# Graph attention in two layers: the store of mask bytes on another queue, a third buffer for it, and two statements moved

## The chip, the cores and the metric

The kernel runs on one core of one Trainium2 chip. The metric is the device time of one execution in microseconds (us); lower is better. Times below are medians of several executions, with the lowest and highest in brackets. PE is the matmul engine, DVE the vector engine, ACT the scalar engine, POOL is GpSimd, and SP is SyncE, which here only starts transfers.

## The reference, cut to what matters

There are 4096 rows of 512 numbers, and a dense 4096 x 4096 matrix `adj` in float32. Layer 0 attends within graphs of 128 rows, layer 1 over all pairs of rows where `adj > 0`.

```python
def _L0_gnn_ref(x, b, edge_encoding, ptr, Wq, bq, Wk, bk, Wv, bv):
    # b and edge_encoding are both adj
    mask = graph_id[:, None] == graph_id[None, :]
    a = jnp.where(mask, query @ key.T * scale, 0.0)
    scores = (a + b + edge_encoding) * jnp.where(mask, 1.0, -1000000.0)
    softmax = jax.nn.softmax(scores, axis=-1) * mask
    return softmax @ value
...
h = jnp.maximum(_layernorm(x), 0.0)
x = x + _L0_gnn_ref(h, adj, adj, ...)
h = jnp.maximum(_layernorm(x), 0.0)
x = x + _L1_gnn_ref(h, adj, ...)        # masks with adj > 0
```

So layer 0 needs from each row of `adj` the 128 entries of its own graph (`diag`) and a sum of exponentials over all the others (`sums`). Layer 1 needs from it one bit for each entry. The kernel reads `adj` once, in layer 0, and leaves the bits as bytes in memory (`a_d`) for layer 1.

## The kernel before

Layer 0 goes through 32 tiles of 128 rows, in pairs g = 0 to 15. `read` does all the work on a tile of `adj`: mask bytes on DVE and their store, `diag` on POOL, the sums on ACT, and the load of the tile three further on. L numbers in profile lines are lines of this kernel, or of the kernel profiled.

```python
def load_adj(pool, i):
    a = pool.tile([P, N], F32, name="a")                 # pool of 3
    nc.sync.dma_start(a, adj[ts(i, P), :])               # L104, 2 MB
...
def norm(src, hn):
    nc.vector.bn_stats(stats, src)                       # L111, "statistics"
    nc.vector.bn_aggr(mv, stats)
    ...                                                  # ve, rstd on POOL
    nc.vector.tensor_scalar(hn, src, mv[:, 0:1], rstd, ALU.subtract, ALU.mult)   # L118
...
def mask_bytes(pool, a, i):
    a8 = pool.tile([P, N], FP8, name="a8")               # pool of 2
    ...
    for u in range(P // B):                              # four operations
        nc.vector.tensor_scalar(a8v[:, u], av[:, u], 0.0, None, ALU.is_gt, saturate=False)  # L133
    nc.gpsimd.dma_start(a_d[i], a8.bitcast(F32))         # L136, 512 KB
...
def read(i, diag, sums):
    mask_bytes(sb, aa[i], i)
    nc.gpsimd.tensor_copy(diag, aa[i][:, ts(i, P)])      # L427
    for c0, c1 in ((0, i * P), ((i + 1) * P, N)):
        nc.scalar.activation(junk[:, c0:c1], aa[i][:, c0:c1], AF.Exp, scale=2.0 * NEG,
                             accum_out=sums[:, n : n + 1])               # L432
    if i + 3 < NT:
        aa[i + 3] = load_adj(ap, i + 3)
...
for g in range(NG):                                      # 16 pairs
    if g + 2 < NG:
        load_pair(g + 2)                                 # L489: xg, 512 KB, pool of 3
    if g == 2:
        w1x = load_w1(pool1, sb)                         # eight DVE operations
    ...
    def look_on(t):                                      # adj of the next pair
        if not last:
            i = G * (g + 1) + t
            nlook[2].append(read(i, nlook[0][:, t, :], nlook[1][t]))
    ...
    look_on(0)
    s = scores(g, hT, gT, r, *look)                      # PE L453, DVE L458, ACT L460
    prepare_on()
    prepare_on()
    if not last:
        ngT = queries(nhT)                               # PE L404, ACT L408
    look_on(1)
    sT = turned(s)                                       # PE L472, ACT L474
    for t in range(G):
        attend(sT, vs[t], g, t)                          # PE L480, DVE L482, ACT starts x's store
        prepare_on()
        if not last:
            nvs.append(values(nhT, t))                   # PE L416, DVE L420
    ...
    if g + 2 < NG:
        nhT, nr = normed(g + 2)                          # statistics, hn, PE L124, ACT L125 (hT)
```

The order of these statements isn't the order in which an engine runs them. The build, which turns this text into one list of instructions for each engine, chooses an order for each list; by what rule it chooses is not shown here.

## Time and profile before

| | kernel before |
|---|---|
| time (3 runs) | 1020.01 us (1017.76 to 1020.05) |
| span of the profiled run | 1017.6 us |
| layer 0, start of scores of pair 0 to pair 12 | 264.8 us |
| from the start of pair 15's scores to the end | 639.2 us |
| clock of PE granted in pairs 0 to 11 | 0.94 |

The page's chain of work that ended last, by engine:

```profile
PE 71%; DMA 12%; DVE 8%; ACT 4%; POOL 3%; issue 1%; ACTq 0%; SPq 0%; DVEq 0%; POOLq 0%
```

Nearly a third of the chain isn't PE, though PE is busy for 94% of the span. The work of PE is there, but at times something else holds it up, and for 12% of the span this chain waited for a transfer (DMA).

### The profile page before, as it was taken

How to read it: one execution, taken by the hardware profiler on the slowest of the kernel's cores; microseconds unless marked ns; L12 is line 12 of the kernel's file. 1: busy time of each engine (PE TensorE's matmuls, PEld its weight loads, DVE VectorE, ACT ScalarE, POOL GpSimd, SP SyncE). 2: the span in 40 equal slices, each digit the busy share in tenths (PEclk: the TensorE clock that was granted, in tenths of full speed). 3: DMA queues.
4: the chain of work that ended last, by engine and by line, in shares of the span. 5: the costliest groups of instructions: out<-in, count | busy, mean ns of one | idle time of the engine just before them, and what ended most of it. 6: DMA issues, size and time to landing. Idle time of an engine off the chain costs nothing.

```text
span 1017.6 us, 12962 instructions
## 1 busy us (share of the span) xinstructions
PE 961.5 (94%) x5051; PEld 826.3 (81%) x5051; DVE 452.8 (44%) x854; ACT 251.0 (25%) x441; POOL 197.2 (19%) x376
## 2 busy tenths in 40 slices
PE   7898889889898999899999999999999999999995
PEld 4475657556576667788899999999999999999995
DVE  3757756556555428755513323323323323323311
ACT  3774745555445212333310000000000000000000
POOL 1211133211112105555511001001001001001000
PEclk9799899999899999999999999999999999999998
DMA  9989988778774114222202123123123122122111
GB/s 354 395 346 365 364 308 308 297 314 300 282 272 166 52 57 130 81 65 65 61 1 84 47 78 83 47 79 83 47 79 83 47 78 84 47 78 82 44 42 34
DMA packets 53431, 148.25 MB, mean 146 GB/s; under 512 B 5874, under 2 KB 22514, under 8 KB 49266
## 3 DMA queue, kind: packets, MB, share of 16 engines
q1 hardware_dynamic: 38962, 113.52, 33.1%
q10 hardware_dynamic: 9792, 17.05, 4.5%
q0 software_dynamic: 4608, 16.78, 4.1%
q8 instruction: 41, 0.67, 0.3%
q14 instruction: 28, 0.23, 0.1%
HBM read 113.77 MB, written 33.55 MB: 145 GB/s over the span
## 4 chain that ended last, share of the span: by engine, by line
PE 71%; DMA 12%; DVE 8%; ACT 4%; POOL 3%; issue 1%; ACTq 0%; SPq 0%; DVEq 0%; POOLq 0%
PE pg L282 48%; PE pp L242 8%; DMA xg<-x 6%; PE pp L416 5%; PE pp L404 4%; DMA a_d<-a 3%; ACT junk L432 3%; DMA a<-adj 3%; PE pp L480 2%; DVE a L133 2%; DVE stats L111 2%; PE pt L124 1%; PE pp L188 1%; POOL rstd L117 1%; DVE x L482 1%
## 5 line engine op out<-in xcount | busy, mean ns | idle before, releaser
L282 PE MATMUL pg<-part,at 128*128 128x348 f32 x3072 | 489.0, 321 | 1.2 <-DVE e L251 1.2
L282 PEld LDWEIGHTS pg<-part,at 128*128 128x128 f32 x3072 | 488.7, 188 | 1.6 <-issue 1.6
L276 DVE CAST at<-at 128x4096 fp32r<-128x4096 fp8e4 x32 | 73.6, 2300 | 311.6 <-PE pg L282 311.6
L289 ACT COPY tot<-pg 128x522 f32<-128x522 f32 x32 | 19.1, 597 | 469.9 <-PE pg L282 469.9
L432 ACT ACTIVATE junk<-a 128x3968 bf16<-128x3968 f32 (+30 forms) x62 | 118.3, 1908 | 37.6 <-DMA a<-adj 21.3
L404 PE MATMUL pp<-hT,m_sb 128*128 128x256 f32 x512 | 118.7, 392 | 9.1 <-ACT hT L125 9.1
L416 PE MATMUL pp<-wv,hT 128*128 128x512 f32 x256 | 123.3, 627 | 2.5 <-ACT hT L125 2.5
L404 PEld LDWEIGHTS pp<-hT,m_sb 128*128 128x128 f32 x512 | 99.9, 198 | 23.9 <-ACT hT L125 9.5
L242 PE MATMUL pp<-w1x,hT 128*128 128x256 f32 (+1 forms) x512 | 118.5, 385 | 0.0
L416 PEld LDWEIGHTS pp<-wv,hT 128*128 128x128 f32 x256 | 51.8, 203 | 69.2 <-issue 66.3
L133 DVE TENSOR_SCALAR a<-a 128x1024 fp8e4<-128x1024 f32 x128 | 87.3, 745 | 46.1 <-DMA a<-adj 23.8
L242 PEld LDWEIGHTS pp<-w1x,hT 128*128 128x128 f32 x512 | 95.6, 192 | 14.0 <-issue 0.5
L582 POOL COPY den_all<-tot 128x1 f32<-128x1 f32 x31 | 5.7, 184 | 368.5 <-DVE tot L290 368.5
L125 ACT ACTIVATE hT<-pt 128x512 f32<-128x512 f32 x64 | 38.2, 600 | 118.1 <-PE pt L124 110.9
L591 POOL TENSOR_TENSOR tot<-tot,row 128x512 f32<-128x512 f32 x31 | 39.9, 1288 | 61.8 <-DVE tot L295 61.8
L480 PE MATMUL pp<-v,sT 128*128 128x512 f32 x64 | 36.8, 657 | 15.3 <-ACT sT L474 15.0
L230 POOL TENSOR_TENSOR part<-e,part 128x522 fp32r<-128x522 f32 x32 | 42.3, 1322 | 29.8 <-ACT part L229 26.2
L136 POOL DMA_DIRECT2D a_d<-a x32 | 22.0, 686 | 117.3 <-DVE a L133 108.1
L482 DVE SCALAR_TENSOR_TENSOR x<-pp,rs_all,xg 128x512 f32<-128x512 f32 x32 | 24.0, 750 | 41.7 <-PE pp L480 41.7
L115 POOL TENSOR_SCALAR ve<-mv 128x1 f32<-128x1 f32 x64 | 18.2, 287 | 121.2 <-DVE mv L113 119.5
L269 DVE STREAM_TRANSPOSE at<-mw 128x1024 f32<-128x1024 f32 x32 | 39.6, 1237 | 0.0
L117 POOL TENSOR_TENSOR rstd<-ve,neghalf 128x1 f32<-128x1 f32 x64 | 38.7, 607 | 3.9
(95 smaller groups left out, 596.6 us busy)
## 6 DMA issues: line engine op xcount, KB each, us to landing
a<-adj SPq DMA_DIRECT2D x32, 2048.0 KB, 11.8
a_d<-a POOLq DMA_DIRECT2D x32, 512.0 KB, 8.8
row<-x_d SPq DMA_DIRECT2D x64, 256.0 KB, 3.4
mw<-a_d SPq DMA_DIRECT2D x128, 128.0 KB, 3.9
xg<-x SPq DMA_DIRECT2D x16, 512.0 KB, 5.5
x_d<-x ACTq DMA_DIRECT2D x32, 256.0 KB, 4.8
out<-tot ACTq DMA_DIRECT2D x31, 256.0 KB, 3.8
wkT_sb<-wkT SPq DMA_DIRECT2D x4, 256.0 KB, 4.0
```

The source lines that it names most:

```text
L117: nc.gpsimd.tensor_tensor(rstd, ve, neghalf, ALU.pow)
L133: nc.vector.tensor_scalar(a8v[:, u], av[:, u], 0.0, None, ALU.is_gt, saturate=False)
L230: nc.gpsimd.tensor_sub(dst[:, :, 1, :], e3, dst[:, :, 0, :].bitcast(F32))
L242: nc.tensor.matmul(pm[g][:, :n], hT[:, k, :], w1x[:, k, g * HW : g * HW + n], start=(k == 0), stop=(k == KC - 1),)
L269: nc.vector.transpose(at8.rearrange("p c n b -> p (c n b)").bitcast(F32).rearrange("p (c u n) -> p c u n", c=NW, n=B), mw.rearrange("p u ( ...
L276: nc.vector.tensor_copy(at.rearrange("p (c b) q -> p c b q", b=BY), at8.rearrange("p c q b -> p c b q"))
L282: nc.tensor.matmul(pg[:, c, : 2 * CW1], at[:, j, :], part(j)[:, c].rearrange("p s w -> p (s w)"), start=(j == 0), stop=(j == NT - 1),)
L404: nc.tensor.matmul(pp[:, : G * P], m_sb[:, k, ts(m, P)], hT[:, k, :], start=(k == 0), stop=(k == KC - 1),)
L416: nc.tensor.matmul(pp, hT[:, k, ts(t, P)], wv[:, k, :], start=(k == 0), stop=(k == KC - 1))
L432: nc.scalar.activation(junk[:, c0:c1], aa[i][:, c0:c1], AF.Exp, scale=2.0 * NEG, accum_out=sums[:, n : n + 1],)
L480: nc.tensor.matmul(po, sT[:, t, :], v, start=True, stop=True)
L591: nc.gpsimd.tensor_add(num, num, row)
```

## The change

There are three edits. The mask bytes get a third buffer. SyncE starts their store in place of GpSimd. And the work on the coming pair's `adj`, which stood ahead of scores and ahead of the turned scores, is moved behind both, in front of the attends. It was meant to let scores and queries go first, and to keep a slow store from blocking the mask operations.

```diff
-        a8 = pool.tile([P, N], FP8, name="a8")
+        a8 = pool.tile([P, N], FP8, name="a8", bufs=3)
...
-        nc.gpsimd.dma_start(a_d[i], a8.bitcast(F32))
+        nc.sync.dma_start(a_d[i], a8.bitcast(F32))
...
-                    look_on(0)
                     s = scores(g, hT, gT, r, *look)
                     prepare_on()
                     prepare_on()
                     if not last:
                         ngT = queries(nhT)
-                    look_on(1)
                     sT = turned(s)
                     nvs = []
                     for t in range(G):
+                        look_on(t)
                         attend(sT, vs[t], g, t)
```

## The prediction

> **What bounds the kernel now.** I read the page first (busy tenths, chain that ended last), then busy time by stretch, then the timeline of PE through layer 0, then the waits and the chain around PE's gaps.
>
> Layer 0 works on pairs of row tiles. For each pair PE runs scores (L453), queries (L404), a transpose of the scores (L472), and twice attend (L480) plus values (L416). DVE turns adj into mask bytes (L133), ACT sums over adj (L432, "junk"). In PE's timeline the score blocks of pairs 0 to 15 start at 57.8, 77.7, 98.0, 124.7, 143.4, 169.2, 192.0, 212.9, 236.6, 255.4, 280.2, 299.5, 322.7, 341.4, 360.1 and 378.4 us. I cut there, at pair 12:
>
> ```profile
> core 0: us, PE busy (x) PEld busy (x) DVE busy (x) ACT busy (x) POOL busy (x), PEclk, DMA share, GB/s
> 57.84:322.65 264.81, 238.09 (x939) 159.16 (x937) 157.62 (x340) 147.72 (x239) 56.53 (x110) 0.94 0.80 306
> 322.65:378.58 55.93, 55.74 (x235) 37.95 (x234) 22.00 (x56) 12.17 (x33) 7.48 (x18) 1.00 0.18 62
> ```
>
> The last three pairs have all of adj on the chip and take 18.70, 18.70 and 18.37 us, PE never idle, clock 1.00. I take 18.7 as PE's floor for a pair. The first twelve take 264.8/12 = 22.1 us: PE has 26.7 us without work and a clock of 0.94, while DVE (60%), ACT (56%) and the DMA engines (80%) all have time left. So **no engine bounds this stretch; waits do**. Above the floor lie 264.8 - 12 x 18.7 = **40.4 us**. That is all the change can win here. What follows 378 us (layer 1, where L282 has PE at 99%) it does not touch.
>
> A pair at the floor, then two that stall (PE's timeline):
>
> ```profile
> 322.65 1.95 PE L453 MATMUL pss<-hT,gT 128*128 128x128 f32 x16
> 324.43 7.07 PE L404 MATMUL pp<-hT,m_sb 128*128 128x256 f32 x32
> ...
> 143.40 1.95 PE L453 MATMUL pss<-hT,gT 128*128 128x128 f32 x16
> 149.57 9.74 PE L404 MATMUL pp<-hT,m_sb 128*128 128x256 f32 x32 [4.22 <-ACT hT L125]
> ...
> 181.31 1.33 PE L480 MATMUL pp<-v,sT 128*128 128x512 f32 x2 [2.54 <-ACT sT L474]
> 182.43 5.13 PE L416 MATMUL pp<-wv,hT 128*128 128x512 f32 x8
> ```
>
> After a gap of 4.22 us the same 32 matmuls of L404 took 9.74 instead of 7.07 us, after 2.54 us L416 took 5.13 instead of 3.60: a gap is paid about one and a half times. The chain of waits tells where the two kinds come from:
>
> ```profile
> 136.64 10.38 DMA a_d<-a
> 147.01 0.03 DVEq L133
> 147.05 0.18 DVE a L133
> 147.22 0.57 DVE v L420
> 147.79 0.67 DVE x L482
> ...
> 148.92 0.60 ACT hT L125
> 149.57 9.75 PE pp L404 x32
> ...
> 165.59 0.76 DVE x L482
> 166.35 0.02 issue
> 166.37 5.64 DMA xg<-x
> 172.01 0.02 issue
> 172.03 1.29 DVE stats L111 x2
> ```
>
> Kind one: DVE stands in front of a mask operation until a store of mask bytes (10.4 us from its issue by POOL) frees one of two buffers; values, attend, ACT's x store and hT queue behind it. Kind two: in DVE's order the statistics of a coming pair (needing xg, loaded only when the last attend frees its buffer) stand ahead of this pair's scores (L458). Scores come 3 us late, ACT's exponentials and junk slide, and sT reaches PE late. The waits of this stretch put sizes to it:
>
> ```profile
> DVE a L133 <- DMA a_d<-a: 20.8, 6, 8.9
> DVE stats L111 <- DMA xg<-x: 15.3, 10, 3.5
> PE pp L480 <- ACT sT L474: 15.0, 9, 3.4
> PE pp L404 <- ACT hT L125: 9.1, 2, 4.9
> ```
>
> **What the Trainium skill says.** "TensorE: Matmul & The Clock Gate", Part 1: an idle window of about 3.4 us drops the array to half clock until it has been busy about as long; the trace agrees in kind (9.74 against 7.07 us), though there a gap of 2.54 us already cost 1.5. "DMA: Bandwidth & Descriptors", "Issuing engines are not separate DMA queues": DMAs of SP, ACT and GpSimd end on the same 16 engines, so the move to SyncE buys no bandwidth. The trace can only agree: stores and loads overlap there. Same page, "Where 436 GB/s comes from": a ceiling of 435 GB/s; the DMA view from 100 to 300 us has single slices up to 450. "Perfetto Trace Analysis", "Optimization Strategy": equal bubbles on the engine that should be full can mean too few buffers, which fits kind one.
>
> **The change, part by part.** No operation is added or removed; PE, DVE and ACT do the same layer-0 work. I compared the instruction order of both builds.
>
> (1) Third buffer for mask bytes. A store may now last until three tiles later, about 1.5 pairs or 28 us, against 2.5 to 12.3 us that stores take. I expect the 20.8 us of DVE waiting to fall under 3. Behind it lay pair 4 (excess 25.75 - 18.7 = 7.1 us) and parts of others.
>
> (2) The adj work behind scores and queries. Before, statistics stand ahead of the scores on DVE in 11 of the 13 pairs 1 to 13; after, in 3 (6, 11, 13). Before, masks run some four pairs ahead of the scores, so POOL's diag copy (three buffers) must wait for a score and the adj loads behind it with it (49.9 us of POOL waiting); after, two to three pairs. Also, the eight operations that build w1x stood before an attend of pair 1, which led to the other large hT stall (pair 2, from 98.0: 26.7 - 18.7 = 8.0 us); after, they follow that pair's attends.
>
> (3) Stores by SyncE. SyncE waits in order, so each store stands ahead of the adj load of its turn. That load needs the same masks done, so it loses nothing; but both stand behind the xg load, which waits for the last attend. From the order: at the attend (about 16.5 us after a pair's scores start) xg, store, load, store, load leave within 2 us. With the two x stores that is 2x2048 + 2x512 + 512 + 2x256 KB = 6144 KB = 6.29 MB a pair; at 390 GB/s (375 at share 0.96 in the first 50 us) 16 us, ending about 14 us into the next pair. The first load is needed about 11 us into that pair and lands at 5 to 7; the second at about 19.6 and lands by 14. Both fit, with 4 to 5 us to spare. At the floor the demand is 6.29 MB/18.7 us = 336 GB/s, under the 350 GB/s that the stretch 58 to 169 us moved.
>
> So what holds PE off its floor goes, and DMA stays just under it. I keep 8 us of the 40.4 for what I cannot see: three pairs with statistics still ahead (1 to 2 us each), w1x in pair 2 (1 us), first pairs and a DMA that runs tight (3 us). Prologue and layer 1: 0. **1020 - (40.4 - 8) = 988 us** (rounded).
>
> **Rivals.**
> - *The wait moves to adj.* For: DMA at 86% of its best rate, loads in one burst behind an in-order SyncE, masks less far ahead, so a late load hits scores sooner (junk stands ahead of the exponentials in several pairs). Against: 4 to 5 us of slack by my schedule. If pairs came at 20.4 us: 12 x (22.1 - 20.4) = 20 us, 1000 us.
> - *ACT stays the brake.* For: a junk operation of about 2 us still stands between the copies of queries and sT in most pairs, and at the floor ACT has 0.4 us between the last query copy and the transpose. Against: pairs 3 and 8 ran at 18.7 and 18.8 us with just such an order. A stall of 1 us in each pair: 996 us.
> - *SyncE's order hurts.* If stores hold back xg or a load holds back the next store, statistics come late and the old wait returns with new names: no gain, about 1015 us. Against: xg leaves first in each burst.
> - *The gain was in DMA alone and is hidden:* no; PE's gaps are on the chain.
>
> **Range and chances.** If all goes: 980. If half of the excess stays: 1000. I take 978 to 1007. Over 2% needs 20.4 of the 40.4 us: 0.79. Within 2%: 0.19. Slower needs new stalls larger than those removed: 0.02.
>
> **What would show it.** Score blocks about 19.3 us apart from pair 0 to 12, pair 15's at about 346 instead of 378 us; PE's waits for hT and sT from 24 to under 8 us; PEclk there 0.98 or more; DVE waiting for a_d under 3 us; DMA near 335 GB/s over the same pairs; the span from pair 15's scores to the end unchanged at 639 us. I am wrong if PE's gaps name adj (through junk or masks) as the releaser, if L404 or L416 still run slow after gaps, or if the time comes from layer 1.

## The result, and the profile after

| | before | after |
|---|---|---|
| time (4 runs each) | 1018.88 us (1016.70 to 1020.05) | 990.44 us (988.49 to 992.32) |
| ratio | | 0.9723, 95% interval 0.9693 to 0.9753 |
| span of the profiled run | 1017.6 us | 990.0 us |
| start of pair 0's scores | 57.84 us | 59.44 us |
| scores of pair 0 to pair 12 | 264.81 us | 235.65 us |
| scores of pair 12 to the end | 694.95 us | 694.91 us |

A ratio here is the mean time of one kernel's runs over the mean of the other's runs of the same rounds, so it isn't quite the ratio of the medians beside it.

The changed kernel is 2.8% faster. The rows of the table add up to the difference of the spans: 29.16 us won in pairs 0 to 11, 1.60 us lost before them, 0.04 us won after. First the chain by engine after the change, then busy time in the first twelve pairs (the columns are those of the same view in the prediction):

```profile
PE 83%; DVE 7%; DMA 3%; ACT 3%; POOL 3%; issue 1%; SPq 0%; ACTq 0%; DVEq 0%
```

```profile
59.44:295.09 235.65, 226.88 (x939) 153.49 (x938) 158.29 (x335) 146.67 (x242) 37.30 (x81) 0.99 0.85 335
```

DMA fell from 12% to 3% of the chain. The same 939 matmuls now take 226.88 us in place of 238.09, with the granted clock at 0.99 in place of 0.94. PE's time without work fell from 26.7 to 8.8 us (235.65 - 226.88). DMA moves 335 GB/s in place of 306, as pairs come faster.

Pairs now start their scores at 59.44, 78.42, 97.30, 116.25, 136.00, 154.70, 173.40, 193.46, 213.46, 233.08, 251.78, 270.48 and 295.09 us. Four of the twelve take 18.70 us, the floor, and three more 18.9 to 19.0. Pairs 3, 6, 7 and 8 are 0.9 to 1.4 us above it. Pair 11 takes 24.61 us and stands out. PE's timeline shows it (start, duration, what; in brackets the idle time ahead and what ended it):

```profile
270.48 1.95 PE L453 MATMUL pss<-hT,gT 128*128 128x128 f32 x16
272.26 7.07 PE L404 MATMUL pp<-hT,m_sb 128*128 128x256 f32 x32
...
283.33 2.08 PE L480 MATMUL pp<-v,sT 128*128 128x512 f32 x2 [2.90 <-ACT sT L474]
285.19 5.76 PE L416 MATMUL pp<-wv,hT 128*128 128x512 f32 x8
```

After a gap of 2.90 us the next blocks run slow: 2.08 and 5.76 us where other pairs have 1.12 and 3.60. The trace has the clock granted at 0.50 there, for 6.83 us from 282.7. So of the 5.9 us that the pair lost, 2.9 are the wait and 3.0 the slow blocks behind it. The waits of the changed kernel from 57 to 323 us (total, times, longest), to be held against those in the prediction; this stretch takes in pair 12 and part of pair 13 too:

```profile
PE pt L124 <- DVE hn L118: 5.4, 6, 1.4
PE pp L480 <- ACT sT L474: 4.3, 2, 2.9
DVE stats L111 <- DMA xg<-x: 3.4, 3, 1.5
```

DVE's wait for `a_d` (20.8 us) and PE's wait for hT (9.1 us) are gone from the list, and the wait for sT fell from 15.0 to 4.3. PE's wait for the normalised rows hn grew from 1.7 to 5.4 us, in six places. The chain of waits through pair 11 tells what held sT:

```profile
266.92 0.76 DVE x L482
...
267.70 0.38 SPq L489
...
268.13 0.46 SPq L136
...
268.75 10.43 DMA a<-adj
...
279.26 3.39 ACT junk L432 x2
...
283.01 0.27 ACT sT L474
```

The last attend of pair 10 (L482) frees a buffer. SyncE then starts the load of xg (L489), the store of mask bytes (L136) and a load of `adj`, in this order. That load lands at 279.2 us. ACT has a sum over this tile in front of the last query copy and of sT, so PE stands still.

What the result doesn't tell is which of the three edits did this. The experiments begin there.

### The profile page after: what moved, and what is told of

Its sections match the earlier page's. It is cut to its first block, busy times and chain, and to the rows that moved or that the text cites. A ratio compares the mean times of both kernels' runs of the same rounds, so it can differ in the third digit from the quotient of the medians.

```text
span 990.0 us, 12907 instructions
## 1 busy us (share of the span) xinstructions
PE 949.5 (96%) x5051; PEld 820.4 (83%) x5051; DVE 456.4 (46%) x854; ACT 251.2 (25%) x441; POOL 176.1 (18%) x344
## 4 chain that ended last, share of the span: by engine, by line
PE 83%; DVE 7%; DMA 3%; ACT 3%; POOL 3%; issue 1%; SPq 0%; ACTq 0%; DVEq 0%
PE pg L282 49%; PE pp L416 11%; PE pp L242 8%; PE pp L404 6%; PE pp L480 3%; PE pss L453 2%; DMA a<-adj 2%; PE pt L124 2%; ACT junk L432 1%; PE pp L188 1%; DVE a L133 1%; DVE stats L111 1%; POOL rstd L117 1%; POOL ve L115 1%; DMA xg<-x 1%
## 5 line engine op out<-in xcount | busy, mean ns | idle before, releaser
L416 PE MATMUL pp<-wv,hT 128*128 128x512 f32 x256 | 119.8, 612 | 2.5 <-ACT hT L125 2.5
L404 PE MATMUL pp<-hT,m_sb 128*128 128x256 f32 x512 | 113.2, 379 | 0.0
L404 PEld LDWEIGHTS pp<-hT,m_sb 128*128 128x128 f32 x512 | 96.1, 190 | 12.9 <-issue 0.5
L416 PEld LDWEIGHTS pp<-wv,hT 128*128 128x128 f32 x256 | 50.3, 197 | 66.1 <-issue 63.2
L133 DVE TENSOR_SCALAR a<-a 128x1024 fp8e4<-128x1024 f32 x128 | 89.6, 749 | 7.2 <-DMA a<-adj 7.2
L115 POOL TENSOR_SCALAR ve<-mv 128x1 f32<-128x1 f32 x64 | 22.4, 354 | 163.3 <-DVE mv L113 161.8
L420 DVE TENSOR_TENSOR v<-pp,bv_sb 128x512 f32<-128x512 f32 x32 | 22.1, 691 | 49.9 <-PE pp L416 49.5
L480 PE MATMUL pp<-v,sT 128*128 128x512 f32 x64 | 34.7, 624 | 4.7 <-ACT sT L474 4.3
L117 POOL TENSOR_TENSOR rstd<-ve,neghalf 128x1 f32<-128x1 f32 x64 | 36.3, 570 | 4.3
L251 DVE TENSOR_TENSOR e<-pp,e 128x256 f32<-128x256 f32 x64 | 26.6, 416 | 22.5 <-ACT e L370 20.1
```

The source lines that it names most:

```text
L117: nc.gpsimd.tensor_tensor(rstd, ve, neghalf, ALU.pow)
L404: nc.tensor.matmul(pp[:, : G * P], m_sb[:, k, ts(m, P)], hT[:, k, :], start=(k == 0), stop=(k == KC - 1),)
L416: nc.tensor.matmul(pp, hT[:, k, ts(t, P)], wv[:, k, :], start=(k == 0), stop=(k == KC - 1))
L480: nc.tensor.matmul(po, sT[:, t, :], v, start=True, stop=True)
```

## The experiments

There were twelve runs, each with five rounds against the kernel before on the same chip. All gave correct results. The last column is the time from the scores of pair 0 to those of pair 15 in the profiled run. At the floor it would be 15 x 18.7 = 280.5 us.

| run | store by | buffers | what else | median, us | ratio to before, 95% interval | 15 pairs, us |
|---|---|---|---|---|---|---|
| before | GpSimd | 2 | | 1018.88 | 1 | 320.6 |
| after | SyncE | 3 | statements moved | 990.44 | 0.9723 (0.9693 to 0.9753) | 292.5 |
| e1_bufs | GpSimd | 3 | | 1011.20 | 0.9922 (0.9900 to 0.9944) | 308.1 |
| e2_sync | SyncE | 2 | | 982.83 | 0.9644 (0.9621 to 0.9668) | 285.0 |
| e3_order | GpSimd | 2 | statements moved | 1018.72 | 0.9986 (0.9963 to 1.0008) | 319.4 |
| e4_bufs_sync | SyncE | 3 | | 988.31 | 0.9690 (0.9669 to 0.9711) | 290.0 |
| e5_gp_sfirst | GpSimd | 2 | statistics behind scores | 993.00 | 0.9736 (0.9711 to 0.9761) | 295.5 |
| e6_gp_sfirst_lead | GpSimd | 2 | the same, masks less far ahead | 1026.77 | 1.0072 (1.0048 to 1.0097) | 327.9 |
| e7_sync_statsfirst | SyncE | 2 | scores behind statistics | 1007.62 | 0.9887 (0.9860 to 0.9914) | 308.6 |
| e8_sync_sfirst | SyncE | 2 | statistics behind scores | 984.25 | 0.9647 (0.9621 to 0.9673) | 288.1 |
| e9_three_hn | SyncE | 3 | masks behind hn | 984.42 | 0.9662 (0.9639 to 0.9684) | 285.6 |
| e10_gp_w1late | GpSimd | 2 | as e5, w1x behind attends | 997.22 | 0.9780 (0.9754 to 0.9806) | 297.4 |
| e11_sync_sums | SyncE | 2 | three sums behind sT | 985.57 | 0.9668 (0.9645 to 0.9692) | 286.7 |
| e12_sync_sums4 | SyncE | 2 | four sums behind sT | 978.73 | 0.9605 (0.9577 to 0.9634) | 280.7 |

### One edit at a time: e1_bufs, e2_sync, e3_order, e4_bufs_sync

The third buffer alone:

```diff
-        a8 = pool.tile([P, N], FP8, name="a8")
+        a8 = pool.tile([P, N], FP8, name="a8", bufs=3)
```

Expected: 

> Only the third mask-byte buffer; the order of instructions is the same as before on all engines. Theory A (order is the main cause): DVE's waits for a_d fall from 20.8 us to under 3, pair 4 loses its 7 us stall, statistics still stand before the scores in 11 pairs: 1009 to 1014 us. Rival B (waits for buffers are the main cause): most of the 28 us gain is here, below 1000 us. Rival C (a store's landing is hidden anyway): 1017 to 1020 us.

The SyncE store alone:

```diff
-        nc.gpsimd.dma_start(a_d[i], a8.bitcast(F32))
+        nc.sync.dma_start(a_d[i], a8.bitcast(F32))
```

Expected: 

> Only the stores moved from GpSimd to SyncE, two buffers. The built order already has the statistics behind the scores in 10 of 13 pairs and masks 1.5 to 2 pairs ahead, as in the changed kernel. Theory A (order is the main cause, and this part makes it): 993 to 1003 us, DVE waiting for a_d perhaps 5 to 10 us. Rival B (as the prediction had it, the moved statements make the order and this part gives nothing): 1015 to 1020 us. Rival D (SyncE's in-order queue costs time): above 1020 us.

The moved statements alone:

```diff
-                    look_on(0)
                     s = scores(g, hT, gT, r, *look)
...
-                    look_on(1)
...
                     for t in range(G):
+                        look_on(t)
                         attend(sT, vs[t], g, t)
```

Expected: 

> Only the adj work moved behind scores and queries in the source; stores by GpSimd, two buffers. The built order still has the statistics before the scores in 11 or more pairs and masks up to 3.4 pairs ahead, as before. Theory A: 1012 to 1020 us. Rival B (the moved statements are what wins): 995 to 1005 us.

The first two edits together. Expected: 

> Third buffer and SyncE, adj work where it was in the source. Theory A: within 5 us of the changed kernel, 988 to 996 us. Rival B: at least half of the gain is missing, above 1004 us.

Measured: the third buffer gives 8 us, the moved statements nothing (the interval holds 1), and the SyncE store 37 us, more than the whole change. The edits don't add up either: a third buffer beside the SyncE store costs 5.5 us (the intervals of e2 and e4 do not meet).

The waits say why. The moved statements alone (e3_order), from 57 to 323 us:

```profile
DVE a L133 <- DMA a_d<-a: 23.5, 7, 9.3
DVE stats L111 <- DMA xg<-x: 12.8, 10, 3.0
```

The SyncE store alone (e2_sync), same stretch:

```profile
DVE stats L111 <- DMA xg<-x: 3.7, 3, 1.4
DVE a L133 <- DMA a_d<-a: 0.8, 3, 0.3
PE pt L124 <- DVE hn L118: 0.2, 1, 0.2
```

Both kinds of stall stay where the statements alone are moved, and both go with the SyncE store alone, even with two buffers. With three buffers and GpSimd (e1_bufs) the wait for `a_d` fell to 1.9 us, while that for xg stayed at 15.7 us; pair 4 fell from 25.75 to 23.00 us and pair 2 from 26.69 to 21.96.

The instruction orders of the builds are plainer still. I compared them on all five engines, leaving out line numbers and the numbers in names. The builds of before, e1 and e3 have the very same order: the moved statements change the text and nothing in what runs, and the 8 us of e1 come from waits that went, and from fewer slow blocks behind them. The changed kernel has the same order as e4, so its two medians, 990.4 and 988.3 us, show how far the same program scatters from one set of runs to another. Their two traces show one way in which it does. In e4's pair 11 PE waits even longer, and no slow block follows:

```profile
282.23 1.12 PE L480 MATMUL pp<-v,sT 128*128 128x512 f32 x2 [3.17 <-ACT sT L474]
283.19 3.60 PE L416 MATMUL pp<-wv,hT 128*128 128x512 f32 x8
```

The clock stays at 1.00 there, and the pair takes 21.80 us, not 24.61. So half of pair 11's loss in the changed kernel's trace isn't a property of the program.

In before, e1 and e3 statistics stand ahead of scores on DVE in 11 of the pairs 1 to 13; in e2, e4 and the changed kernel in 3 (pairs 6, 11 and 13). Such a place is no stall by itself: pairs 3 and 8 of the kernel before have it too and took 18.71 and 18.81 us.

So it is the edit of the store's engine after which the build lays DVE out in another way. But that is so far only a coincidence of two things, as the store itself also changed: on its new queue it lands in 6.4 us (median over the whole run) instead of 8.8.

### Order or queue: e5_gp_sfirst, e6_gp_sfirst_lead, e7_sync_statsfirst, e8_sync_sfirst

Theory Q says that the SyncE store wins because of the order of instructions that comes with it. Theory H says that it's the store's own queue and speed. Theory L says that what counts is how far the masks run ahead of scores (up to 3.4 pairs before, 1.5 to 2.5 with SyncE; the prediction's "four" and "two to three" count the pair itself as well). The first run keeps GpSimd and two buffers, and only gives the build an edge for its ordering, a rule that the operations of a block may not stand ahead of a named one of the same engine. Here the block is all that DVE does in `normed(g + 2)`, statistics, hn and the rest:

```diff
-                        nhT, nr = normed(g + 2)
+                        with tc.issue_after(s_ins[-1].ins):   # s_ins: the DVE operations of L458
+                            nhT, nr = normed(g + 2)
```

Expected: 

> The kernel before (GpSimd store, two buffers), with one edge more for the instruction order: on DVE the statistics of pair g+2 may not stand ahead of the scores of pair g. Theory Q (SyncE's store wins only because the builder then orders DVE in another way; what counts is statistics behind scores): most of the gain of the SyncE store without SyncE, so 990 to 1003 us, DVE's wait for xg in front of the scores gone and PE's wait for sT from 15 to under 6 us; the wait for a_d stays. Theory H (the queue of the store itself, quick landing without POOL, does it): 1010 us or more, as the third buffer alone. Theory L (what counts is how far masks run ahead): masks still lead by 3.5 pairs here, so little, 1008 to 1020.

Measured: 993.0 us. With GpSimd, two buffers and nothing moved in the text, 27 of the 37 us are there. PE's wait for sT fell from 15.0 to 7.1 us (under 6 was expected). The stores, still started by GpSimd, land in 6.4 us here as well, so their quick landing doesn't need the new queue; but e5 alone can't tell the order from the quick landing. DVE's timeline of pair 5 shows the edge at work. The kernel before, in which PE began these scores at 169.15 us:

```profile
172.03 1.29 DVE L111 BATCH_NORM_STATS2 stats<-xg 128x6 f32<-128x512 f32 x2 [2.32 <-DMA xg<-x]
...
173.92 0.40 DVE L458 SCALAR_TENSOR_TENSOR s<-diag,pss 128x256 f32<-128x256 f32 x1
```

And e5_gp_sfirst, in which PE began them at 161.86 us:

```profile
165.00 0.40 DVE L458 SCALAR_TENSOR_TENSOR s<-diag,pss 128x256 f32<-128x256 f32 x1
165.32 0.68 DVE L111 BATCH_NORM_STATS2 stats<-xg 128x6 f32<-128x512 f32 x1
```

Before, DVE idled for 2.32 us until xg had landed. The scores behind it were ready at 171.10, when PE's block of 1.95 us ended, and DVE took them 4.8 us after PE had begun (173.92 - 169.15). In e5 it takes the scores after 3.1 us and does the statistics next, with no wait. The pair took 22.9 us before (169.15 to 192.02) and takes 19.0 now (161.86 to 180.84).

The second run adds that the masks of pair g+1 may not stand ahead of the scores of pair g-1:

```diff
-                            nlook[2].append(read(i, nlook[0][:, t, :], nlook[1][t]))
+                            with tc.issue_after(s_ins[-2].ins) if len(s_ins) > 1 else nullcontext():
+                                nlook[2].append(read(i, nlook[0][:, t, :], nlook[1][t]))
```

Expected: 

> GpSimd store, two buffers, the edge of the run before, and a second: the masks of pair g+1 may not stand ahead of the scores of pair g-1, so that masks lead by 1.5 pairs, somewhat less than in the build with the SyncE store (1.5 to 2.5). Theory Q: 983 to 1000, near the run before. Theory L: here first the large gain, 983 to 1000, with the run before left at 1008 or more. Theory H: stays at 1005 or more, and DVE still waits over 10 us for a_d.

Measured: 1026.8 us, slower than before. Theories Q and L had at most 1000. Theory H's "1005 or more" and its wait for `a_d` (24.0 us) fit, but H had 1010 or more for e5, which ran at 993.0. ACT now waits 76.7 us for `adj` and SyncE 192.4 us for masks before it can start the next loads. Held back masks mean late loads. Theory L falls in this form, and with it the hope that a shorter lead is good in itself. The SyncE builds run well with a lead of 1.5 to 2.5 pairs, so how much lead a build can do with depends on the rest of its order.

The third run is the reverse. It has the SyncE store, but scores stand behind the statistics of pair g+2 (which are now written ahead of the scores; `st_ins` holds the operations of L111):

```diff
+                    if g + 2 < NG:
+                        ahead2 = normed(g + 2)
+                        behind = tc.issue_after(st_ins[-1].ins)
-                    s = scores(g, hT, gT, r, *look)
+                    with behind:
+                        s = scores(g, hT, gT, r, *look)
...
-                        nhT, nr = normed(g + 2)
+                        nhT, nr = ahead2
```

Expected: 

> The reverse: SyncE store, two buffers, but the scores of every pair are forced to stand behind the statistics of pair g+2 on DVE. Theory Q: the gain of the SyncE store (37 us) is mostly lost, 1000 to 1012 us, with 15 us or more of DVE waiting for xg and PE waiting for sT in most pairs. Theory H and theory L (masks lead by 1.5 to 2.5 here): it stays within 8 us of the SyncE store alone, 983 to 991.

Measured: 1007.6 us. The quick store is still there (6.5 us to landing), and 25 of the 37 us are lost. PE's waits from 57 to 323 us (line numbers are two higher in this kernel):

```profile
PE pp L482 <- ACT sT L476: 11.4, 13, 2.6
PE pt L126 <- DVE hn L120: 5.7, 7, 1.5
```

PE waits 13 times for sT, once in each of pairs 0 to 12. So a quick store without the order isn't enough. The edit has a side effect: it also moved PE's transposes for coming pairs ahead of those of the scores, so part of the loss may be theirs.

The fourth run adds the edge of e5 to the SyncE store. Expected: 

> SyncE store, two buffers, statistics forced behind scores in all pairs (alone, 3 pairs of 13 still have them ahead: 6, 11 and 13). Theory Q: those three pairs come to the floor of 18.7 us; pairs 6 and 11 lost 1.3 and 3.1 us there, so 3 to 5 us faster than the SyncE store alone, about 979. Theories H and L: no change, 983 within 2 us.

Measured: 984.3 us, nothing gained (3 to 5 us were expected). PE still waits for sT in pairs 6 and 11, 1.51 and 3.07 us. So the statistics still ahead of scores in those pairs weren't what delayed sT there.

What follows: theory Q carries most of the gain, shown from both sides: 27 us won without SyncE, 25 us lost with it, of which an unknown part is e7's side effect. Which operation of the order carries how much isn't separated, since the edge of e5 moves others on DVE along with the statistics. What the store's queue may do by itself is left with some 10 us: e5 lacks that to e2, and e7 is 12 us faster than before with the order turned round.

### What the third buffer costs: e9_three_hn

With three buffers beside the SyncE store, a mask operation of a coming tile stands between statistics and hn on DVE in each of pairs 2 to 14; with two buffers (e2_sync) it does in 6 of them. In e4_bufs_sync, as in the changed kernel, PE waits 5.4 us for hn in six places, and 4.8 us for sT. The edge added to it puts masks behind hn; one of those pairs keeps a mask operation there:

```diff
-                            nlook[2].append(read(i, nlook[0][:, t, :], nlook[1][t]))
+                            with tc.issue_after(hn_ins[-1 if t and g < 8 else -3].ins):
+                                nlook[2].append(read(i, nlook[0][:, t, :], nlook[1][t]))
```

Expected: 

> SyncE store and three mask-byte buffers, as in the run of the two together (988.3 us, against 982.8 us with two buffers), with edges for the instruction order alone: mask operations of a coming tile may not stand between the statistics of a pair and its normalisation (hn) on DVE, where the third buffer had let them move. Theory O (the third buffer costs 5.5 us beside the SyncE store because masks pulled ahead delay hn, for which PE's transposes wait 5.4 us): 980 to 984 us, PE's wait for hn under 1 us. Theory B (the third buffer costs in another way, by longer or clashing stores or the prologue): 987 to 990.

Measured: 984.4 us, and the wait for hn is gone from the list; only the waits for sT (5.4 us) and one of 0.2 us are left. The 15 pairs went from 290.0 to 285.6 us, the figure of two buffers. The two ratios' intervals just overlap, so the 4 us rest on the trace as well as on the times. No cost of the third buffer by itself is left to see (285.0 us in e2); what costs is the freedom it gives to place masks where they delay hn.

### The 10 us that e5 lacks: e10_gp_w1late

In e5, pair 2 took 27.3 us, with 5.3 us of waiting for hT. That is most of what e5 lacks: of the 10.5 us by which its 15 pairs are longer than e2's, 8.5 lie in pair 2 (27.34 against 18.84). The chain led back to the eight operations that build w1x, which stand ahead of the attends of pair 1 there. The edge puts them behind:

```diff
-                        w1x = load_w1(pool1, sb)
+                        w1x = load_w1(pool1, sb, x_ins[-1])   # its DVE operations behind this attend
```

Expected: 

> GpSimd store, two buffers, statistics forced behind scores (993.0 us alone), and one edge more: the eight operations that build w1x stand behind the attends of pair 1 and not ahead of them. In the run before, pair 2 still took 27.3 us, with a wait of 5.3 us for hT that the chain leads back to them. Theory Q (order alone carries the gain of the SyncE store): 983 to 987 us, pair 2 under 20 us, so that a GpSimd kernel with two buffers comes within 4 us of the SyncE store. Rival: the 10 us between the two are the waits for the store itself (a_d, 10.1 us of DVE waiting there), and it stays at 990 to 993.

Measured: 997.2 us, a miss. Pair 2 still takes 26.8 us (97.60 to 124.41), and PE waits 4.90 us for hT. ACT's timeline, pair 1 to 2:

```profile
94.89 1.16 ACT L435 ACTIVATE junk<-a 128x1152 bf16<-128x1152 f32 x1 [6.09 <-DMA a<-adj]
...
103.82 0.58 ACT L125 ACTIVATE hT<-pt 128x512 f32<-128x512 f32 x1
```

ACT stands for 6.09 us at a sum whose load hasn't landed, then does the sums of two tiles, then hT. In all GpSimd builds except e6 the sums of two tiles (9 and 10) stand ahead of this hT; in the SyncE builds, e7 apart, that of one (tile 8). The w1x operations were on the chain, but they weren't what made it long. Whether the sums' place alone explains pair 2, and how much of the 10 us is the wait for `a_d` (10.1 us of DVE in e5), was not tried. Two hints lie in the traces. In e1, with the order of the kernel before, the third buffer alone took pair 2 to 21.96 us, where the same order with two buffers had 26.69 (before) and 24.38 (e3). And in e5 SyncE waits 53.1 us for POOL's copies of `diag`, which hold the buffers of `adj`, before it can start loads of `adj`, and ACT waits 22.9 us for `adj`; in e2 the first wait is not in the list and the second is 6.7 us.

### What is left in pairs 6 and 11: e11_sync_sums, e12_sync_sums4

In ACT's order, pairs 6 and 11 of the SyncE builds are the ones with a sum over a late tile (18 and 29) directly ahead of the last query copy and sT. The edges put these two sums, and that of tile 20 in pair 7, behind sT, on top of e2_sync:

```diff
+                            with tc.issue_after(sT_ins[{18: 6, 20: 7, 29: 11}[i]].ins) if i in (18, 20, 29) else nullcontext():
-                            nc.scalar.activation(
+                                nc.scalar.activation(
```

Expected: 

> SyncE store, two buffers (982.8 us), and for ACT's order one edge for each of three sums over adj (tiles 18, 20 and 29): they stand behind the copy of sT of pairs 6, 7 and 11 and not ahead of it. Theory J (what is left in pairs 6 and 11, PE's waits of 1.4 and 2.8 us for sT, comes from a sum that waits for its adj load ahead of the last query copy): pairs 6 and 11 come to within 0.5 us of 18.7, 976 to 979 us. Rival: the late load then holds up hT or the next sum instead, and the stall moves: 981 to 985.

Measured: 985.6 us, just above what the rival expected, but with a lesson. Pairs 6 and 11 came to 18.7 us, and all of the stall went to pair 12, to the sum of the last tile:

```profile
297.78 1.83 PE L481 MATMUL pp<-v,sT 128*128 128x512 f32 x2 [4.46 <-ACT sT L475]
```

The last run adds `31: 12` to the table. Expected: 

> The run with the moved sums (985.6 us, where pairs 6 and 11 came to 18.7 us but PE's wait for sT went to pair 12, 4.5 us, behind the sum of tile 31), with one edge more: the sum of tile 31 stands behind the copy of sT of pair 12. Theory J: every pair comes to 18.7 to 19 us and PE waits under 1 us for sT; 977 to 980 us, the fastest of all. Rival: the wait for the last adj load only moves on to pair 13 (hT stands behind that sum), and it stays at 983 to 986.

Measured: 978.7 us, the lowest median of all, 1.2% under the changed kernel by the ratios (0.9605 against 0.9723). The intervals of e12 and e2 overlap, so the 4 us between them rest on the trace as well. The 15 pairs take 280.7 us, the floor, and PE's busy time by stretch shows it full:

```profile
57.60:285.00 227.40, 226.54 (x957) 154.94 (x957) 156.93 (x335) 146.25 (x238) 43.30 (x81) 1.00 0.87 343
```

PE is without work for 0.9 us of 227.4, and the clock is 1.00. Theory J holds: statistics still stand ahead of scores in pairs 6, 12 and 13 of this build, and those pairs take 18.7 to 18.8 us. It also shows that DMA, at 343 GB/s, can feed PE at its floor.

## Why the prediction was right or wrong

**Right in the total: 988 predicted, 990.4 measured.** The reading of the bound held: all of the gain is in pairs 0 to 11, and from pair 12 on the time is the same (694.95 and 694.91 us; pair 12 lost 1.1 us and the time from pair 15 on won as much). The floor of 18.7 us a pair is real, as e12 reaches it. PEclk is 0.99 (0.98 or more predicted), DMA 335 GB/s as predicted, PE's waits for hT and sT 4.3 us (under 8), DVE waits no more for `a_d` (under 3). The stretch from pair 15's scores to the end is 638.1 us (639). That the gain was found is no luck, as the order was read from the whole build, whichever edit makes it. That the total came so close is in part luck: of the causes listed for the 8 us kept back, few came, and others took their place.

**The residue was somewhat small.** Over the floor remain 235.65 - 12 x 18.7 = 11.3 us where 8 were kept, and the prologue lost 1.6 where 0 was put. Pair 11 has 5.9 of the 11.3 us, pairs 3, 7 and 8 together 3.3, pair 6 1.4, and the first three 0.7. So the pairs come 19.64 us apart and not 19.3, and pair 15's scores start at 351.9 and not at 346.

**Part (1), the third buffer: right alone, wrong in the sum.** e1 takes the wait for `a_d` to 1.9 us and wins 8 us, and the prediction had 7.1 in pair 4 and parts of others; in e1's trace pair 4 won 2.8 and pair 2 4.7. But beside the SyncE store two buffers were enough (0.8 us of waiting in e2), and the third then cost 5.5 us through PE's wait for hn. The prediction had no term for that wait, though the change in order was there to be read.

**Part (2), "the adj work behind scores and queries": the step that failed.** The prediction put the new order, statistics ahead of scores in 3 pairs and not in 11, to the moved statements. The order itself was read rightly from the two builds, and its worth too (e5, e7). But only the build with all three edits was compared with the one before. The moved statements alone leave every engine's order and the time as they were (e3), and beside the two other edits they change no order either (e4); the SyncE store alone gives the new order (e2). Built one edit at a time, the same comparison would have told this ahead of any run.

**The w1x term in part (2) failed as well.** Pair 2 lost its 8.0 us in the changed kernel, as predicted, but with w1x moved behind the attends in e10, on top of e5, it kept a stall of 4.90 us. The same part had POOL's `diag` copies holding up the loads of `adj`. SyncE's wait for them did go (29.7 us before, 0.4 after), though POOL itself waits longer for scores (49.9 before, 69.0 after).

**Part (3), "Stores by SyncE ... it loses nothing": the term with the wrong size.** It was sized at zero. The edit is worth 37 us, because of the order that the build makes around it.

**The residue's cause was misread.** The prediction gave "three pairs with statistics still ahead (1 to 2 us each)". Pair 6 lost 1.4, pair 11 lost 5.9, pair 13 nothing. In e8 the statistics stand behind in all pairs, and pairs 6 and 11 stall as before; in e12 the sums stand behind sT, and no pair stalls. So it was the first rival, "the wait moves to adj", in a small form. The schedule in part (3) had the first load landing 5 to 7 us into the pair and needed 11 us in. In pair 11 it landed 8.7 us in (279.18 - 270.48). As the 3.4 us sum stood ahead of the last query copy, whose matmuls ended about 279.3, it was needed about 5.4 us in. The prediction named such a pair among its signs of being wrong: a gap of PE that leads to `adj` through a sum, and L416 slow after it. Both came, in one pair of twelve. Nor was the price of a gap steady: put at one and a half times its length, it was twice in the changed kernel's pair 11 (5.9 for 2.90 us) and once in e4's (3.1 for 3.17 us). The figure of the second rival, 996 us, can't be rebuilt from its text: twelve stalls of 1 us over the floor make 992, and paid one and a half times 998.

**Open:** why the build orders DVE otherwise when the store stands on SyncE; the 10 us between e5 and e2; and when a gap of PE brings the half clock.

## What to carry to other kernels

When an edit changes the instruction order, build each of its parts alone and compare the orders before putting the gain to a part: here a change of queue reordered other engines, and the moved statements moved no instruction. Then look, on each engine that runs its queue in order, for an operation that waits for a load and stands ahead of a ready operation on the critical path; one edge that puts it behind was worth 27 us in e5, and four edges on top of e2_sync 4 us in e12. A further buffer isn't free either, since it lets work move ahead of what is urgent; and a stall that is removed in one place can move to the next such operation, so follow it to the last one.

## What the Trainium skill lacked or had wrong

- "DMA: Bandwidth & Descriptors", "Issuing engines are not separate DMA queues", says that starting DMAs on more engines only saves time on the sequencer that starts them. As to bandwidth no run here contradicts it (306 GB/s before, 335 after, in step with the pace). But the move of 32 stores alone took the time from 1019.9 to 982.8 us (e2), and the page doesn't say that the queue chosen can change the order in which a build lays out the other engines. The median from issue to landing of these stores fell too, from 8.8 to 6.4 us; but it fell as far in e5, where GpSimd still starts them.
- "TensorE: Matmul & The Clock Gate", Part 1, puts the idle window that slows the array at about 3.4 us. Here shorter gaps were enough at times: after 2.44 us in e10 the block behind the next one took 5.17 instead of 3.60 us, after 2.90 us in the changed kernel 5.76, both with a granted clock of 0.50. Yet gaps of 2.83 us (e2) and 3.17 us (e4) left it at 3.60 us and the clock at 1.00. So in these traces the length of a gap alone doesn't tell whether the clock falls. Between 55 and 400 us each such stretch lasted 3.41 or 6.83 us, once 10.24 (e6).
- "Perfetto Trace Analysis", "Optimization Strategy", says that equal bubbles can mean too few buffers. A third buffer gave 8 us with the store on GpSimd (e1) and cost 5.5 us with it on SyncE (e4 against e2).
- "PSUM — Partial Sum Buffer", "Engine vs sequencer instructions", says that the queues of ScalarE, VectorE and GpSimdE are strict FIFO. The trace agrees: in pair 11 sT stood behind a sum that waited for its load, and PE lost 2.90 us. No page that I read says that a build may lay out such an operation ahead of one that is ready: statistics ahead of scores in 11 of 13 pairs before, in 3 after.
